# Layer 0 attention: scores of two key tiles, then the products of the last two

## Chip, cores and metric

One core of a Trainium2 chip runs the whole program. The metric is device time in microseconds (us) of one execution. Before the change it is 3277.91 us, the median of 3 runs (3275.79 to 3279.31).

## What is computed

The program is two layers: a convolution-and-attention block (layer 0) on 8 images of 256 channels and 32x32 pixels, then an attention and expert layer on the same data (layer 1). The change is in the softmax attention of layer 0, which for each image has 4 heads of 32 query and key channels and 64 value channels over 1024 pixels:

```python
qkv = _bn(_conv1x1(x, qkv_w), qkv_g, qkv_b, qkv_m, qkv_v)
qkv = qkv.reshape(B, NH, 2 * KD + HD, N)
q, k, v = (qkv[:, :, :KD], qkv[:, :, KD:2 * KD], qkv[:, :, 2 * KD:])
attn = jnp.einsum('bhkn,bhkm->bhnm', q, k) * SCALE
attn = jax.nn.softmax(attn, axis=-1)
out = jnp.einsum('bhdm,bhnm->bhdn', v, attn).reshape(B, Cc, H, W)
pe = _bn(_dwconv3(v_img, pe_w), pe_g, pe_b, pe_m, pe_v)
out = out + pe
```

The rest of layer 0 is a norm, a 1x1 convolution to 1024 channels, a 3x3 depthwise convolution, a gated product, a 1x1 convolution back and a filter on 8x8 blocks in the frequency domain.

## The kernel before

**Attention of one image** (`attend(b)`, from L725). The 1024 queries go in 4 chunks of QC = 256, the keys in NT = 8 tiles of 128, so an image has 32 steps (chunk, key tile). A step writes the scores of all 4 heads into one PSUM tile `s` (4 matmuls of 128x256, one for each head), ScalarE takes the exponential into `pT` in SBUF, and `product` multiplies the `pT` of the step before with v (8 matmuls into `po`, 32 columns each, so four can stand side by side in the array) and with ones (4 such matmuls into `sm`, for the sums of the softmax). The products are thus one step late. In the profile these are `s<-qst,kst`, `pT<-s`, `po<-pT,vT` and `sums<-pT,ones`.

**Close of a chunk** (`close`): ScalarE copies `po` to `pu` and `sm` to `ss`, then, as small steps in the list `todo` of which each step of the loop takes one (`later()`): `invert` (reciprocal `sr` on VectorE), `split` (`rh` on ScalarE, `rl` on GpSimd) and `spread` (4 matmuls `rb` on TensorE, then two VectorE operations, `pu<-pu,rb` and `o<-o,pu`).

**Other work beside it.** `main_of(i)` weaves into the steps of `attend(i)` the second norm of image i-1 (`norm2`), the frequency filter of image i-2 (`spectrum`: `pz`, `zf`, `pf`, `gf`, `py`) and the first norm and q, k of image i+1 (`queries_keys`: `nsum`, `ms`, `tr`, `rbn`, `pq`). `together` adds the depthwise convolutions as a side stream: for every microsecond that the main stream names in its `yield`, side steps worth 1.0 us (0.5 in image 0) are issued. A side step is one tap of the convolution on VectorE (`conv<-hpad`, `x<-hpad`, `o<-vpad`, 1.3 us each in its `yield`); after the third and fifth tap of a group the next group is opened: two matmuls `ph` into one PSUM bank, and two ScalarE evictions (into `hpad` and into the group's start).

**Order.** All engines here are called through `InOrder`, which keeps each engine's instructions in the order in which the Python program issues them. So the yields decide who stands behind whom in each engine's queue.

**Buffers.** PSUM has `ps_s` with 2 tiles of 2 banks (`s`, but also `pz` and others), `ps_o` with one `po` and one `sm`, and `ps_m` with 2 single banks (`ph`, `pq`, `pf`, `py`, `rb`, `rbn`, `ms`, `nsum`, `tr` and others). `pT` has 2 buffers. A tile that takes a buffer waits until the last reader of the tile that had it is done.

**End of an image** (`ending`): value products and transposes, projection, rest of the last close. After the last image comes a tail of layer 0 (to about 1400 us), then layer 1, which the change doesn't touch.

Of the kernel before, what the change touches and what calls it, by code (L numbers as in the profile page):

```python
# [9 lines left out]
F32 = mybir.dt.float32  # L10
F32R = mybir.dt.float32r
BF16 = mybir.dt.bfloat16
AF = mybir.ActivationFunctionType
# [5 lines left out]
P = 128  # L19
# [4 lines left out]
NH, KD, HD = 4, 32, 64  # L24
# [4 lines left out]
QC = 256  # L29
# [44 lines left out]
def conv_attn_hybrid_kernel(  # L74
# [351 lines left out]
    pe, act, dve, pool = (InOrder(tc, e) for e in (nc.tensor, nc.scalar, nc.vector, nc.gpsimd))  # L426
    t = [None] * B
    with ExitStack() as l0:
        wpool = l0.enter_context(tc.tile_pool(name="w0", bufs=1))
        one = l0.enter_context(tc.tile_pool(name="one0", bufs=1))  # L430
        two = l0.enter_context(tc.tile_pool(name="two0", bufs=2))
        ps_s = l0.enter_context(tc.tile_pool(name="ps_s0", bufs=2, space=PSUM))
# [289 lines left out]
        def attend(b):  # L722

            qst, kst, vT = (att[b][n] for n in ("qst", "kst", "vT"))
            nj = NT
            todo = []

            def product(po, sm, j, pT):  # L730


                for pair in range(NH // 2):
                    for i in range(4):
                        ch = pair * P + i * KD
                        pe.matmul(
                            po[i * KD : (i + 1) * KD, pair, :],
                            vT[:, j, ch : ch + KD],
                            pT[:, ch // HD, :],
                            start=(j == 0 and pair == 0),  # L740
                            stop=(j == nj - 1 and pair == 1),
                        )
                for hd in range(NH):
                    pe.matmul(
                        sm[hd * KD : (hd + 1) * KD, :], ones[:, :KD], pT[:, hd, :], start=(j == 0), stop=(j == nj - 1)
                    )

            def close(c, po, sm):
                pu = two.tile([P, NH // 2, QC], F32, tag="pu", name="pu", bufs=1)
                act.copy(pu, po)  # L750
                ss = two.tile([P, QC], F32, tag="ss", name="ss", bufs=1)
                act.activation(ss, sm, AF.Copy, accum_out=accs[:, 0, b, c : c + 1])
                r = two.tile([P, QC], F32, tag="sr", name="sr", bufs=1)
                rh = two.tile([P, QC], F32R, tag="rh", name="rh", bufs=1)
                rl = two.tile([P, QC], F32R, tag="rl", name="rl", bufs=1)
                qs = slice(c * QC, (c + 1) * QC)

                def invert():
                    dve.reciprocal(r, ss)

                def split():
                    act.activation(rh, r, AF.Copy, accum_out=accs[:, 1, b, c : c + 1])
                    pool.tensor_sub(rl, r, rh.bitcast(F32))

                def spread():
                    rb = ps_m.tile([P, NH // 2, QC], F32, tag="mm", name="rb")
                    for pair in range(NH // 2):
                        pe.matmul(rb[:, pair, :], pick_r[:, pair, :], rh, start=True, stop=False)
                        pe.matmul(rb[:, pair, :], pick_r[:, pair, :], rl, start=False, stop=True)
                    o = att[b]["o"][:, :, qs]  # L770
                    dve.tensor_mul(pu, pu, rb)
                    dve.tensor_add(o, o, pu)

                return [None, invert, None, split, None, None, spread]

            def later():
                if todo:
                    step = todo.pop(0)
                    if step:
                        step()  # L780

            late = None
            for c in range(N // QC):
                qs = slice(c * QC, (c + 1) * QC)
                po = ps_o.tile([P, NH // 2, QC], F32, tag="po", name="po")
                sm = ps_o.tile([P, QC], F32, tag="sm", name="sums")
                for j in range(nj):
                    ks = slice(j * P, (j + 1) * P)
                    s = ps_s.tile([P, NH, QC], F32, tag="s", name="s")
                    for hd in range(NH):  # L790
                        pe.matmul(s[:, hd, :], kst[:, hd, ks], qst[:, hd, qs], start=True, stop=True)
                    pT = two.tile([P, NH, QC], F32, tag="pT", name="pT")
                    act.activation(pT, s, AF.Exp)
                    if late:
                        product(*late[:4])
                        if late[2] == nj - 1:
                            todo = close(c - 1, *late[:2])
                    late = (po, sm, j, pT)
                    later()
                    yield 2.4  # L800
            product(*late)
            todo = close(c, po, sm)
            att[b]["rest"] = todo
            yield 1.3

# [224 lines left out]
        def weave(main, side, every, rest=True):  # L1030

            for n, us in enumerate(main):
                yield us
                if n % every == every - 1:
                    step = next(side, None)
                    if step is not None:
                        yield step
            if rest:
                yield from side

        def none():
            yield from ()

        def later_on(n, steps):
            for _ in range(n):
                yield 0.0
            yield from steps
# [35 lines left out]
        def main_of(i):  # L1083

            steps = attend(i)
            if i >= 1:
                head = weave(norm2(i - 1), spectrum(i - 2) if i >= 2 else none(), 1)  # L1090
                yield from weave(head, steps, 3, rest=False)
            later = queries_keys(i + 1) if i + 1 < B else none()
            yield from weave(steps, later_on(2, weave(set_up(), later, 1) if i == 0 else later), 2)
            if i + 1 < B:
                stack(i + 1)
                yield from ending(i)
            else:
                yield from weave(project(i, (0,)), weave(finish(i), gelu_steps(i - 1), 1), 1)
                yield from project(i, (1,))
# [4 lines left out]
        steps = queries_keys(0)  # L1104
# [22 lines left out]
        product, take, turn = values(0)  # L1127
# [10 lines left out]
        def set_up():  # L1138

            fold(projw, proj_s, KC, "diag_p")  # L1140
            yield 1.0
            through(piw, "n2b", 2 * ng, pi_o)
            dve.tensor_mul(dw_o, pi_o, dw_w[:, :, 4])
            yield 3.5
            fps = ps_m.tile([P, HALF], F32, tag="mm", name="fps")
            pe.matmul(fps[:, :C], sel, fp, start=True, stop=True)
            dve.tensor_copy(filt, fps[:, :C])
            yield 0.5
# [32 lines left out]
        head = weave(norm2(B - 1), spectrum(B - 2), 1)  # L1181
# [131 lines left out]
    with ExitStack() as l1:  # L1313
        wpool = l1.enter_context(tc.tile_pool(name="w1", bufs=1))
        one = l1.enter_context(tc.tile_pool(name="one1", bufs=1))
        two = l1.enter_context(tc.tile_pool(name="two1", bufs=2))
        tiny = l1.enter_context(tc.tile_pool(name="tiny1", bufs=4))
        ps_s = l1.enter_context(tc.tile_pool(name="ps_s1", bufs=2, space=PSUM))
# [136 lines left out]
        done, late, ready, turns, pr_of, pT = set(), [], [], [], {}, {}  # L1455
# [61 lines left out]
        def product(b, qc):  # L1517
            po = ps_m.tile([P, KC, QC], F32, tag="mm", name="po1")
            nj = (qc + 1) * nq
            w = pT.pop((b, qc))  # L1520
            for g in range(KC):
                for j in range(nj):
                    c0 = max(0, j * P - qc * QC)
                    pe.matmul(
                        po[:, g, c0:], v_of[b][:, j, g * P : (g + 1) * P], w[:, j, c0:], start=(j == 0), stop=(j == nj - 1)
                    )
                yield 0.43 * nj
            tb = t[b][:, :, qc * QC : (qc + 1) * QC]
            dve.tensor_add(tb, tb, po)
            done.add((b, qc))  # L1530
# [50 lines left out]
    with ExitStack() as l2:  # L1581
# [162 lines left out]
        def close(h, b, c):  # L1744

            t = ts.pop((h, b))
            dve.tensor_add(c[:, 0:2, :], c[:, 0:2, :], c[:, 7:8, :].to_broadcast([P, 2, QC]))
            dve.tensor_add(c[:, 2:4, :], c[:, 2:4, :], c[:, 1:2, :].to_broadcast([P, 2, QC]))
            dve.tensor_add(c[:, 2, :], c[:, 2, :], c[:, 6, :])
            dve.tensor_add(c[:, 4, :], c[:, 4, :], c[:, 3, :])  # L1750
            dve.tensor_add(c[:, 6, :], c[:, 6, :], c[:, 3, :])
            t4 = t.rearrange("p k (c n) -> p (k c) n", n=QC)
            dve.tensor_add(t4, t4, c[:, 0::2, :])
            nc.sync.dma_start(ov[b][:, :, cut(h)], t)
# [62 lines left out]
        for n in range(len(pieces) + LAG3):  # L1817
            one_ = two_ = three = iter(())
            if n < len(pieces):
                h, b, e = pieces[n]  # L1820
                i = n // NE
# [141 lines left out]
```

## Time and profile before

| | us |
|---|---|
| median of 3 runs | 3277.91 |
| the profiled execution | 3277.43 |
| its span, first to last instruction | 3275.3 |
| layer 0 with its tail | about 1400 |
| one image in the middle (key loads of two images 160.5 apart) | 160.5 |
| in one such image: TensorE busy | 150.95 |
| VectorE busy | 135.41 |
| ScalarE busy | 88.75 |

A window of the trace gives the busy time of each engine in it; the timeline gives the instructions one after the other, with the idle time of the engine before each and the instruction that ended this idle time. Matmul ends in the trace are modelled and overlap the next start, so distances from start to start are what counts on TensorE.

### The profile page before, as it was taken

How to read it: one execution, taken by the hardware profiler on the slowest of the kernel's cores; microseconds unless marked ns; L12 is line 12 of the kernel's file. 1: busy time of each engine (PE TensorE's matmuls, PEld its weight loads, DVE VectorE, ACT ScalarE, POOL GpSimd, SP SyncE). 2: the span in 40 equal slices, each digit the busy share in tenths (PEclk: the TensorE clock that was granted, in tenths of full speed). 3: DMA queues.
4: the chain of work that ended last, by engine and by line, in shares of the span. 5: the costliest groups of instructions: out<-in, count | busy, mean ns of one | idle time of the engine just before them, and what ended most of it. 6: DMA issues, size and time to landing. Idle time of an engine off the chain costs nothing.

```text
span 3275.3 us, 43158 instructions
## 1 busy us (share of the span) xinstructions
PE 3047.3 (93%) x17218; PEld 2050.7 (63%) x17218; DVE 2417.4 (74%) x3796; ACT 1438.2 (44%) x2227; POOL 327.9 (10%) x472
## 2 busy tenths in 40 slices
PE   7997999999999997779999998899999999999999
PEld 4554555555555554346556665678787777787787
DVE  5388888888888886735555444688888878888887
ACT  4554555555555553223333322444444444444443
POOL 2110212111111100011222111000000000000000
PEclk9998999999999999889999999999999999999999
DMA  3202020202020200031111101200000100000000
GB/s 111 53 1 52 27 52 27 53 27 52 27 52 27 52 14 20 4 136 44 50 61 51 39 26 72 75 20 20 20 20 20 33 20 20 20 20 26 20 7 13
DMA packets 49831, 121.45 MB, mean 37 GB/s; under 512 B 7302, under 2 KB 20054, under 8 KB 45782
## 3 DMA queue, kind: packets, MB, share of 16 engines
q1 hardware_dynamic: 49622, 118.61, 11.6%
q8 instruction: 137, 2.24, 0.3%
q14 instruction: 72, 0.59, 0.1%
HBM read 48.20 MB, written 37.88 MB: 26 GB/s over the span
## 4 chain that ended last, share of the span: by engine, by line
PE 48%; DVE 6%; ACT 1%; issue 1%; POOL 1%; DMA 0%; SPq 0%; ACTq 0%; POOLq 0%; DVEq 0%
PE pm L68 13%; PE pa L68 12%; PE q L68 12%; PE s L68 4%; PE po L68 3%; PE pv L68 2%; PE pk L68 2%; DVE nm L68 1%; DVE pr L68 1%; DVE zt L68 1%; DVE st L68 1%; ACT pr L68 1%; PE tp L68 1%; PE tpz L68 1%; PE tpt L68 1%
## 5 line engine op out<-in xcount | busy, mean ns | idle before, releaser
L68 ACT ACTIVATE h<-h,bn_o,bn_s 128x512 f32<-128x512 f32 x384 | 308.7, 813 | 627.7 <-DVE h L68 627.6
L68 DVE SCALAR_TENSOR_TENSOR x<-hpad,vec,x 128x1024 f32<-128x1024 f32 x248 | 320.4, 1297 | 32.1 <-ACT x L68 25.9
L68 DVE SCALAR_TENSOR_TENSOR conv<-hpad,vec,conv 128x1024 f32<-128x1024 f32 x256 | 331.5, 1301 | 14.3 <-ACT conv L68 8.4
L68 PE MATMUL pm<-h,w 128*128 128x512 f32 (+1 forms) x768 | 321.5, 528 | 0.0
L68 ACT ACTIVATE pT<-s 128x1024 f32<-128x1024 f32 x256 | 261.5, 1024 | 128.1 <-PE s L68 127.0
L68 PE MATMUL po<-pT,vT 128*32 128x256 f32 x4096 | 276.7, 388 | 12.0 <-ACT pT L68 11.3
L68 PE MATMUL ph<-xn,piw 128*128 128x512 f32 x512 | 250.8, 615 | 22.7 <-ACT conv L68 14.2
L68 PE MATMUL s<-kk,z 128*128 128x512 f32 x512 | 242.0, 600 | 0.6 <-DVE pr L68 0.6
L68 PE MATMUL s<-qst,kst 128*128 128x256 f32 x1024 | 216.5, 334 | 0.0
L68 PEld LDWEIGHTS s<-qst,kst 128*128 128x128 f32 x1024 | 146.5, 191 | 88.5 <-issue 82.2
L68 PEld LDWEIGHTS pm<-h,w 128*128 128x128 f32 x768 | 146.9, 191 | 76.6 <-issue 62.6
L68 DVE TENSOR_TENSOR h<-pa,first 128x512 f32<-128x512 f32 x128 | 88.3, 689 | 136.0 <-PE pa L68 134.3
L68 ACT ACTIVATE hpad<-ph,pi_o 128x512 f32<-128x512 f32 x126 | 87.0, 690 | 228.5 <-PE ph L68 228.4
L68 DVE TENSOR_TENSOR h<-h,wb 128x1024 f32<-128x1024 f32 x128 | 156.2, 1221 | 41.0 <-ACT h L68 41.0
L68 DVE SCALAR_TENSOR_TENSOR o<-vpad,pe_w,o 128x1024 f32<-128x1024 f32 x128 | 163.6, 1283 | 17.4 <-ACT o L68 14.7
L68 DVE TENSOR_TENSOR h<-h,first 128x256 f32<-128x256 f32 x384 | 163.2, 425 | 13.2
L68 PEld LDWEIGHTS ph<-xn,piw 128*128 128x128 f32 x512 | 88.9, 190 | 132.1 <-issue 89.1
L68 PE MATMUL pz<-pow__117,hid 128*128 128x256 f32 x512 | 129.2, 408 | 44.4 <-DVE hid L68 44.4
L68 PEld LDWEIGHTS po<-pT,vT 128*32 128x32 f32 x4096 | 107.5, 109 | 97.1 <-ACT pT L68 15.2
L68 PE MATMUL sums<-pT,ones 128*32 128x256 f32 x2048 | 158.7, 382 | 0.0
L68 PE MATMUL pa<-tz,ws 128*128 128x256 f32 x512 | 155.0, 385 | 3.8 <-DMA ws<-sums_d 3.8
L68 PE MATMUL q<-t,ws 128*128 128x256 f32 x512 | 152.8, 380 | 0.8 <-DVE t L68 0.8
(279 smaller groups left out, 5870.6 us busy)
## 6 DMA issues: line engine op xcount, KB each, us to landing
td<-t SPq DMA_DIRECT2D x8, 1024.0 KB, 3.8
t<-td SPq DMA_DIRECT2D x8, 1024.0 KB, 4.8
te<-ud SPq DMA_DIRECT2D x16, 512.0 KB, 4.0
out_dram<-te SPq DMA_DIRECT2D x16, 512.0 KB, 2.8
ze<-zd SPq DMA_DIRECT2D x15, 512.0 KB, 3.9
t<-in_x_dram SPq DMA_DIRECT2D x7, 1024.0 KB, 6.3
qst<-hi SPq DMA_DIRECT2D x56, 128.0 KB, 2.3
qst<-lo SPq DMA_DIRECT2D x56, 128.0 KB, 2.3
```

What stands on the lines that cost most here:

```text
L68: return self._tc.keep_in_program_order(method(*args, **kwargs))
```

## The change

The loop goes over pairs of key tiles. The scores of both tiles are issued first; then come, tile by tile, the products of a tile of the last pair and the exponential of the new tile. The yield is 4.8 instead of 2.4 for each tile, so that side work comes between pairs and not between tiles. The list `todo` is shortened so that `spread` still comes at about the same tile, and the weaving counts are adapted (6 norm steps for each pair instead of 3 for each tile, and every step of the loop instead of every second).

```diff
-                return [None, invert, None, split, None, None, spread]
+                return [None, invert, split, spread]
...
-            late = None
+            late = []
...
-                for j in range(nj):
-                    ks = slice(j * P, (j + 1) * P)
-                    s = ps_s.tile([P, NH, QC], F32, tag="s", name="s")
-                    for hd in range(NH):
-                        pe.matmul(s[:, hd, :], kst[:, hd, ks], qst[:, hd, qs], start=True, stop=True)
-                    pT = two.tile([P, NH, QC], F32, tag="pT", name="pT")
-                    act.activation(pT, s, AF.Exp)
-                    if late:
-                        product(*late[:4])
-                        if late[2] == nj - 1:
-                            todo = close(c - 1, *late[:2])
-                    late = (po, sm, j, pT)
+                for j0 in range(0, nj, 2):
+                    pair = []
+                    for j in (j0, j0 + 1):
+                        ks = slice(j * P, (j + 1) * P)
+                        s = ps_s.tile([P, NH, QC], F32, tag="s", name="s")
+                        for hd in range(NH):
+                            pe.matmul(s[:, hd, :], kst[:, hd, ks], qst[:, hd, qs], start=True, stop=True)
+                        pair.append((j, s))
+                    last, late = late, []
+                    for i, (j, s) in enumerate(pair):
+                        if last:
+                            product(*last[i])
+                        pT = two.tile([P, NH, QC], F32, tag="pT", name="pT")
+                        act.activation(pT, s, AF.Exp)
+                        late.append((po, sm, j, pT))
+                    if last and j0 == 0:
+                        todo = close(c - 1, *last[1][:2])
                     later()
-                    yield 2.4
-            product(*late)
+                    yield 4.8
+            for step in late:
+                product(*step)
             todo = close(c, po, sm)
+            todo.insert(2, None)
...
-                yield from weave(head, steps, 3, rest=False)
+                yield from weave(head, steps, 6, rest=False)
...
-            yield from weave(steps, later_on(2, weave(set_up(), later, 1) if i == 0 else later), 2)
+            yield from weave(steps, later_on(1, weave(set_up(), later, 1) if i == 0 else later), 1)
```

## The prediction

> **What bounds the kernel now.** I read the page first, then a table of windows for one image in the middle of layer 0, then the timeline inside it.
>
> ```profile
> PE 3047.3 (93%) x17218; PEld 2050.7 (63%) x17218; DVE 2417.4 (74%) x3796; ACT 1438.2 (44%) x2227; POOL 327.9 (10%) x472
> ```
> ```profile
> 450.40:610.90 160.50, 150.95 (x1216) 85.71 (x1214) 135.41 (x129) 88.75 (x134) 26.51 (x32) 0.99 0.15 40
> ```
>
> The columns of the second are window, length, then busy us of PE, PEld, DVE, ACT, POOL, clock, DMA share, GB/s. PE is busy 94% of an image and DVE 84%: either can set the time, in different stretches. The next lines, the PE timeline of a stretch of image 0 without side work, price a step.
>
> ```profile
> 61.14 0.74 PE L68 MATMUL s<-qst,kst 128*128 128x256 f32 x4
> 61.81 1.07 PE L68 MATMUL po<-pT,vT 128*32 128x256 f32 x16
> 62.70 0.61 PE L68 MATMUL sums<-pT,ones 128*32 128x256 f32 x8
> 63.24 0.74 PE L68 MATMUL s<-qst,kst 128*128 128x256 f32 x4
> 63.91 1.07 PE L68 MATMUL po<-pT,vT 128*32 128x256 f32 x16
> ```
>
> Start to start: a step takes 63.24 - 61.14 = 2.10. Where scores follow scores they start 0.115 apart (eight in 44.21 to 45.13), so four stream 0.46, yet `po` starts 0.67 after them: 0.21 is lost going from 128*128 to 128*32. `po` streams 0.89. `sums` followed by `nsum`, which is 128*32 too, takes 0.43 (76.27 to 76.70), followed by scores 0.54: 0.11 lost going back. So a change of shape and back costs 0.32, and 2.10 = 0.46 + 0.21 + 0.89 + 0.43 + 0.11.
>
> The third view is the timeline of all engines in that middle image.
>
> ```profile
> 546.89 0.69 DVE L68 TENSOR_TENSOR pu<-pu,rb 128x512 f32<-128x512 f32 x1 [2.94 <-PE rb L68]
> ...
> 576.12 0.69 DVE L68 TENSOR_TENSOR pu<-pu,rb 128x512 f32<-128x512 f32 x1 [1.16 <-PE rb L68]
> ...
> 596.45 1.29 DVE L68 TENSOR_TENSOR hid<-x,conv 128x512 f32<-128x512 f32 x2
> 597.77 0.78 ACT L68 ACTIVATE conv<-ph,dw_o,vec 128x512 f32<-128x512 f32 x1 [2.60 <-DVE hid L68]
> 598.60 1.98 PE L68 MATMUL ph<-xn,piw 128*128 128x512 f32 x4 [2.84 <-ACT conv L68]
> ```
>
> Until the first `rb` PE is late and DVE waits for it (2.94); afterwards DVE is full and in the end PE waits for DVE, through ACT (2.84). So the path of a middle image is PE up to the first `rb`, DVE from there to `hid`, then both.
>
> **What the Trainium skill says.** "TensorEngine Tiling (Array Packing)", Tiling Modes: a change of tiling mode drains the array. The 0.32 above agrees. "TensorE: Matmul & The Clock Gate", Architectural detail: ScalarE and VectorE are strict FIFO; so what stands behind a waiting exponential waits too. The trace of before shows ACT evictions and exponentials in issue order only. "Perfetto Trace Analysis", Identifying the Most-Contended Engine: matmul busy time is no measure of headroom. It holds here: the 94% contain the 0.32s.
>
> **The change part by part.** No arithmetic is added or removed: 1024 `s`, 2048 `po`, 1024 `sums` matmuls and 256 exponentials stay. The order in which the two programs stand on each engine shows what moves.
>
> *Shape changes.* 32 for each image become 16: 16 x 0.32 = 5.1 for each image, 41 in all. This is a gain of PE alone.
>
> *A new wait, of the exponentials.* With two `pT` buffers the exponential of a tile takes the buffer that the product just before it reads. Before, that product had been issued a whole step earlier. Now the second exponential starts only when the second product is done. From the trace: PE to ACT takes about 0.25 after the last stream (`nsum` to `part`, 77.13 to 77.38), the exponential 1.02, ACT to PE 0.04 (50.81 to 50.85). With E the end of a pair's products, it ends at E + 1.28. The next pair's second scores overwrite the scores it reads; with no side work they would start at E + 0.11 + 0.46. They wait 0.74. Side work of X us on PE between pairs shrinks this to 0.74 - X. Behind the waiting exponential stand, on ACT, the evictions of `ph`, `pq`, `ms`, the copies of the close and so on; PE waits for these where a third `ps_m` tile is wanted.
>
> *Walk of a middle image*, t = 0 at its first `pz` (475.73 in the profile), with `ph` or `pq` 1.72, `pz` 3.45, `pf` 0.86, `py` 0.95, pair of products 2.66:
> - Head. The two score tiles now come after six norm steps. The third `pz` takes the buffer of the first scores: waits 0.6 for the exponential. Second `tr`: before, scores and products stood ahead of it; now only `pf` and `rbn`. The POOL chain for it takes 5.56 + 3.77 (484.90 to 490.46 to 494.23) from t = 8.7, so it comes at 18.1 and not 16.8: 1.3. The last `pf` waits 0.7 for an eviction. First pair of products ends 23.5, second 39.9.
> - Pair 3: one `ph`, `py`, `ph` ahead, ends 48.9. Pair 4 has nothing ahead: 0.74, ends 53.6. Before, the same eight products ended at 51.7.
> - Then `ph`; `ph nsum`; `ph ms nsum ph`. In the last, `nsum` needs the bank of `ph`, evicted behind the exponential: 1.3. First `rb` starts at 75.1. Before: 70.4. The difference: waits 4.7, one more `ph`, `nsum`, `ms` and scores ahead of it 2.9, shape changes -2.2.
> - DVE takes `pu` at 75.8 instead of 71.2 (+4.6). From there to `hid` it has 29 taps of 1.29, two `sr` of 1.75, two double `xn` of 1.40, two `lo` of 0.75, two `pu`,`o` of 1.38: 48.0. Before it took 49.55 (one tap more, one wait of 1.16). So `hid` is 3.0 late.
> - After `hid` PE has one `ph` less to do (issued earlier), fewer shape changes and not the wait for `pT` of 1.21 at 604.37; DVE has 21.1 of work to its last `sr`, where before it took 23.6 with its waits. -2.4.
> Sum: +0.6. I took every hand-over at its shortest; up to the first `rb` six new ones stand on PE's path, and at an estimated 0.1 each (PE to ACT took 0.25 above, and 0.34 from the end of the `nsum` at 550.94 to its `part` at 551.71) the image comes to +1.2. Five such images: +6.0.
>
> *Image 0.* DVE has slack, PE sets the time: 16 x -0.32 = -5.1, and the short gaps between pairs (`sps` 0.47, none, `nsum` 0.43, `fps` 0.43, `tr`, `rbn tr`, `rbn`) bring waits of 0.28, 0.74, 0.31, 0.3, 0.55, 0.3, 0.3; sum 2.8. About -2.4.
>
> *Image 1.* All its norm steps now precede the scores, and the first exponentials stand bare; three gaps are empty or one `nsum`. The first close's `sr`, on which DVE waits already (5.79 before), comes at 186.8 instead of 183.5, the first `ph` evictions later still, and DVE is full from 204 to 262. +3.2.
>
> *Image 7.* No q and k of a next image: no third `ps_m` tile. First `rb` +1.1, one tap fewer behind it -1.3, hand-overs 0.6: +0.4. Its four bare gaps lie where DVE sets the pace.
>
> *Edits at nothing.* The shorter `todo` puts `spread` at tiles 22 and 23 where it was at 22; `insert(2, None)` leaves `finish` as it was. If the cover goes (DVE waiting in front of `sr`), a pair's period, 4, is the price. SP's transfers keep their order; `qst` and `kst` loads move with the image.
>
> Sum: 6.0 - 2.4 + 3.2 + 0.4 = +7.2. On the profiled execution 3277.43 (span 3275.3 and 2.1 around it) this is 3284.6; on the median, 0.5 above it, 3285.
>
> **Unknown costs, from both sides.** Per middle image: walk without allowance +0.6; if the head's waits fall into DVE's slack (up to 2.6, `tr` and `pf` and `pz`) -2.0; if instead two more evictions hold a bank as `nsum`'s does, +3.8. I take +1.2. Image 1: +1 to +5. Image 0: -3.5 (half the gaps hidden) to -1.
>
> **Rivals.**
> - *The waits only change places* (forecast): 3277 to 3295, at 3285. Chance 0.60, of which 0.20 lies within 0.2% of the time before.
> - *The shape changes come through* (faster). PE is at 94% in the page. 41 less the gaps that are too short (3 + 2 + 5 x 0.8 + 3 = 12) is 29, and about half where DVE sets half the path: 3263. Place: PE up to the first `rb` of each image. It decides if that `rb` comes no more than 1.2 later than before, since DVE's stretch behind it is shorter by 1.5. Against it: the extra `ph` ahead of it alone costs 1.7. Chance 0.15.
> - *ACT becomes the bottleneck in order*: exponentials stand behind an eviction that waits for DVE (`hpad` for the taps of the group before), and scores behind the exponential; 4 for each of 8 images: 3310. For: such waits exist (2.60 above). Against: ACT is busy 55%. Chance 0.15.
> - *Nothing moves*: DVE's 135 of 160 hide all of it: 3278. Against: DVE waits for PE at `rb`. Chance 0.10.
>
> **How the numbers follow.** Something under 0.2% (6.6 us) can't be told from no change here. Slower: 0.40 of the forecast and 0.15 of the third, 0.55. Same: 0.20 + 0.10 = 0.30. Faster 0.15. The forecast's own range is 3277 to 3295; with half of the rivals' reach on each side 3268 to 3302 holds 8 in 10.
>
> **What would show it.** Right: `s` in runs of 8 and about 0.32 less PE for each two steps; DVE's wait at the first `pu<-rb` grows from 2.94 to about 5 in middle images; PE waits of `s` for ACT `pT` of up to 0.74; `tr` for POOL `r` 1.3; image period 161 to 163. Wrong: a period under 159, or that `pu` wait gone (second case); exponentials waiting for ACT evictions over 1 each (third). If image 0 isn't shorter, the price of a shape change is not what I took.

## The result, and where it went

The changed kernel takes 3288.15 us in the median of 12 runs (3283.96 to 3294.37), the kernel before 3278.97 beside it (12 runs, 3273.93 to 3282.12). Ratio 1.0029, 95% interval 1.0022 to 1.0037: slower by 0.3%, 9.2 us. Forecast were 3285 and 7.2 us more.

The first profile of the changed kernel fell on its slowest execution (3294.37, span 3292.6, mean clock 0.969). Its page has these rows in place of those shown of before: the engines, and the two groups that the change concerns (busy us, mean ns | idle time before them).

```profile
PE 3033.9 (92%) x17218; PEld 2076.5 (63%) x17218; DVE 2412.5 (73%) x3796; ACT 1440.9 (44%) x2225; POOL 309.3 (9%) x472
...
L68 ACT ACTIVATE pT<-s 128x1024 f32<-128x1024 f32 x256 | 260.8, 1024 | 249.9 <-PE sums L68 248.4
...
L68 PE MATMUL s<-qst,kst 128*128 128x256 f32 x1024 | 187.7, 326 | 9.6 <-ACT pT L68 9.4
```

The same two groups in the kernel before:

```profile
L68 ACT ACTIVATE pT<-s 128x1024 f32<-128x1024 f32 x256 | 261.5, 1024 | 128.1 <-PE s L68 127.0
...
L68 PE MATMUL s<-qst,kst 128*128 128x256 f32 x1024 | 216.5, 334 | 0.0
```

PE is busy 13 us less, for the same 17218 matmuls, and the time is longer. Exponentials now wait for `sums`, the last matmuls of a product, and no longer for `s`; scores wait 9.4 us for exponentials, where they waited for nothing.

A second execution (label after_again below: 3287.09, span 3285.4) lies near the median and is used for the account. The next two views are tables of windows, one window for each image, bounded by the last `t<-pp` of an image. Columns as in the prediction: window, length, busy us of PE, PEld, DVE, ACT, POOL, clock, DMA share, GB/s. First the kernel before: image 0, a middle image, image 7, and the tail of layer 0.

```profile
40.00:150.59 110.59, 104.73 (x1065) 60.19 (x1067) 42.79 (x46) 58.95 (x89) 8.11 (x18) 0.98 0.25 58
...
636.40:796.85 160.45, 150.90 (x1213) 85.71 (x1212) 135.44 (x128) 88.75 (x134) 26.51 (x32) 0.99 0.15 40
...
1117.72:1261.19 143.47, 132.16 (x1131) 76.22 (x1130) 126.63 (x118) 75.68 (x108) 12.87 (x18) 0.98 0.03 12
1261.19:1398.50 137.31, 103.84 (x359) 62.29 (x358) 94.98 (x96) 36.59 (x64) 4.32 (x14) 0.91 0.03 10
```

The same of after_again, with one middle image more:

```profile
40.00:150.41 110.41, 100.96 (x1064) 61.69 (x1066) 42.25 (x47) 58.64 (x90) 7.26 (x18) 0.98 0.25 58
...
632.16:792.43 160.27, 146.56 (x1213) 87.50 (x1212) 134.51 (x129) 89.50 (x135) 23.16 (x32) 0.99 0.15 40
952.70:1116.00 163.30, 149.56 (x1213) 88.38 (x1212) 134.51 (x129) 89.50 (x135) 23.15 (x32) 0.97 0.15 40
1116.00:1263.22 147.22, 130.75 (x1131) 78.41 (x1130) 126.05 (x117) 74.04 (x106) 12.96 (x18) 0.94 0.03 12
1263.22:1404.30 141.08, 105.36 (x359) 62.99 (x358) 96.24 (x97) 36.63 (x64) 4.33 (x14) 0.90 0.02 10
```

A middle image has 4.3 us less of PE and takes as long as before (160.27 to 160.45). Image 6 takes 3 us more than images 3 to 5 although it does the same work on every engine: its clock is 0.97 and not 0.99. Image 7, the tail and the untouched rest of the program (1876.8 before, 1881.1 now, span less the end of the tail) are 3.7, 3.8 and 4.3 longer. Of these the prediction had only +0.4 for image 7.

So the clock has to be looked at. These are windows of 3.41 us of after_again in the head of image 3:

```profile
484.73:487.29 2.56, 2.56 (x13) 2.04 (x12) 2.52 (x3) 0.26 (x1) 2.48 (x3) 1.00 0.00 0
487.29:490.70 3.41, 1.61 (x8) 0.68 (x6) 3.41 (x5) 0.73 (x3) 2.19 (x7) 1.00 0.00 0
490.70:494.11 3.41, 3.41 (x16) 3.36 (x16) 2.36 (x4) 0.00 (x0) 0.00 (x0) 0.50 0.00 0
494.11:497.53 3.42, 3.42 (x54) 1.97 (x52) 1.93 (x2) 1.39 (x2) 0.00 (x0) 1.00 0.02 5
```

and these of before in the ending of image 3:

```profile
627.45:630.87 3.42, 1.11 (x9) 0.64 (x6) 3.39 (x6) 2.25 (x5) 0.00 (x0) 1.00 0.92 209
630.87:634.28 3.41, 3.17 (x4) 1.51 (x5) 0.09 (x1) 0.04 (x1) 0.00 (x0) 0.50 0.61 137
634.28:637.69 3.41, 3.41 (x12) 2.09 (x11) 1.51 (x3) 1.29 (x2) 0.00 (x0) 1.00 0.00 0
```

The clock is full or half for a whole window. The windows lie on a fixed grid: the half-clock windows of images 3 and 6 of before start at 630.87 and 1112.15, 141 windows apart, which makes 3.4133 each. In both places the window of half clock comes after one in which PE had little to do (1.61 and 1.11 us). If PE bounds such a window, it costs half of PE's busy time in it, at most 1.7 us; so for each stretch I take half of PE's busy time in its half-clock windows as what the clock costs there, and call the remainder its length at full clock. This is an estimate, too high where PE isn't the bound.

| | before: length, clock's part, at full clock | after_again |
|---|---|---|
| image 0, from 40 | 110.6, 1.7, 108.9 | 110.4, 1.7, 108.7 |
| image 1 | 137.2, 4.6, 132.7 | 136.3, 4.1, 132.2 |
| image 2 | 188.1, 5.9, 182.2 | 185.1, 3.0, 182.1 |
| images 3 to 5, each | 160.5, 1.6, 158.9 | 160.3, 1.7, 158.6 |
| image 6 | 160.4, 1.6, 158.9 | 163.3, 4.7, 158.6 |
| image 7 | 143.5, 2.2, 141.2 | 147.2, 5.1, 142.1 |
| tail of layer 0 | 137.3, 8.2, 129.1 | 141.1, 9.7, 131.4 |
| rest of the program | 1876.8, 24.0, 1852.8 | 1881.1, 27.4, 1853.7 |

Of the 10.1 us between the two spans, the clock's part is about 8, and about 2 remain at full clock: the images up to 6 gain 2, image 7, the tail and the rest lose 4. These are two single executions. In the fourteen profiles of this case the untouched rest lasts from 1877 to 1883 us, and 1881 in a kernel with the tail and the rest of before (before_filled below); how much of its 4.3 belongs to the change is not known. That the account holds, and that the clock follows PE's idle time, was argued so far; the experiments with added matmuls tested it.

### The profile page after: what moved, and what is told of

Its sections match the earlier page's. It is cut to its first block, busy times and chain, and to the rows that moved or that the text cites. A ratio compares the mean times of both kernels' runs of the same rounds, so it can differ in the third digit from the quotient of the medians.

```text
span 3292.6 us, 43182 instructions
## 1 busy us (share of the span) xinstructions
PE 3033.9 (92%) x17218; PEld 2076.5 (63%) x17218; DVE 2412.5 (73%) x3796; ACT 1440.9 (44%) x2225; POOL 309.3 (9%) x472
## 4 chain that ended last, share of the span: by engine, by line
PE 48%; DVE 6%; ACT 1%; POOL 1%; issue 1%; DMA 1%; SPq 0%; POOLq 0%; ACTq 0%; DVEq 0%
PE pm L68 12%; PE pa L68 12%; PE q L68 11%; PE s L68 4%; PE po L68 3%; PE pv L68 2%; PE pk L68 2%; DVE nm L68 1%; DVE pr L68 1%; DVE zt L68 1%; DVE st L68 1%; ACT pr L68 1%; PE tp L68 1%; DVE h L68 1%; PE tpz L68 1%
## 5 line engine op out<-in xcount | busy, mean ns | idle before, releaser
L68 PE MATMUL s<-qst,kst 128*128 128x256 f32 x1024 | 187.7, 326 | 9.6 <-ACT pT L68 9.4
L68 PEld LDWEIGHTS s<-qst,kst 128*128 128x128 f32 x1024 | 143.5, 200 | 55.9 <-issue 31.8
L68 PEld LDWEIGHTS po<-pT,vT 128*32 128x32 f32 x4096 | 121.4, 111 | 87.5 <-issue 6.5
L68 PE MATMUL pa<-tz,ws 128*128 128x256 f32 x512 | 157.1, 389 | 3.4 <-DMA ws<-sums_d 3.4
L68 PE MATMUL pa<-tz,w 128*128 128x256 f32 x512 | 153.6, 383 | 0.0
```

Source lines behind the costliest of these rows:

```text
L68: return self._tc.keep_in_program_order(method(*args, **kwargs))
```

## The experiments

Every ratio is to the kernel before, run on the same chip beside the experiment (medians 3279.5 to 3280.0).

**Three pT buffers.**

```diff
-        pow_ = wpool.tile([P, HID // P, C], F32, name="pow_")
-        nc.sync.dma_start(pow_, po_wT.rearrange("(k p) o -> p k o", p=P))
+        pow_ = piw.rearrange("p k (g o) -> p (k g) o", o=C)
...
-                        pT = two.tile([P, NH, QC], F32, tag="pT", name="pT")
+                        pT = two.tile([P, NH, QC], F32, tag="pT", name="pT", bufs=3)
```

> The changed kernel with three pT buffers; to find the room, the weights of the 1x1 convolution back (pow_) are left out and slices of piw stand in for them. The second exponential of a pair then waits for the first product of the pair and no longer for the second. Theory of the prediction (the new wait takes the place of what the shape changes give): the waits of the scores for pT (9.4 us in all) go, evictions behind the second exponential come up to 1.3 earlier, the first rb of a middle image comes 2 or more earlier and DVE's wait at the first pu falls from 6 to under 4; 1 to 2.5 us for each image, ratio to the kernel before 0.995 to 0.999. Rival (the hold of the buffer matters little; the lost time lies in how side work is grouped and in image 0): under 4 us in all, ratio 1.001 to 1.003.

3280.86 us, ratio 1.0002 (0.9996 to 1.0009). The view is ACT's table of waits in the first 1320 us: waited for, us in total, times, longest. Three buffers:

```profile
ACT pT L68 <- PE sums L68: 73.0, 101, 2.4
ACT pT L68 <- PE s L68: 59.2, 41, 4.5
```

The changed kernel (after_again):

```profile
ACT pT L68 <- PE sums L68: 245.3, 219, 6.7
```

The wait is the buffer's, and it cost 7 us (3288.15 to 3280.86), more than the rival allowed and less than the theory asked for. The load of weights that this kernel leaves out is no part of it: the first scores come at 44.6 us, in after_again at 44.0. At full clock image 0 is 105.2 instead of 108.7, image 7 139.7 instead of 142.1, but a middle image 157.8 instead of 158.6. The first `pu` of a middle image came 0.8 earlier, not 2: that step of the theory fell. The middle images are 161.0 to 164.0 long, more than in the changed kernel, because they have 2 to 4 half-clock windows each; that took part of the gain.

**The order of before in the portions of the change.**

```diff
                 for j0 in range(0, nj, 2):
-                    pair = []
                     for j in (j0, j0 + 1):
...
-                        pair.append((j, s))
-                    last, late = late, []
-                    for i, (j, s) in enumerate(pair):
-                        if last:
-                            product(*last[i])
                         pT = two.tile([P, NH, QC], F32, tag="pT", name="pT")
                         act.activation(pT, s, AF.Exp)
-                        late.append((po, sm, j, pT))
-                    if last and j0 == 0:
-                        todo = close(c - 1, *last[1][:2])
+                        if late:
+                            product(*late[0])
+                            if late[0][2] == nj - 1:
+                                todo = close(c - 1, *late[0][:2])
+                        late = [(po, sm, j, pT)]
                     later()
                     yield 4.8
```

> The changed kernel with its yields and weaving, but the instructions of a pair in the order of before: scores, exponential, product of the tile before, for each of the two tiles in turn. So the grouping of the side work, the shorter list and the weaving counts stay, the shape changes of before come back, and the new wait is gone. Theory of the prediction (shape changes are worth 5.1 for each image on PE, and PE sets the time up to the first rb and after hid): slower than the changed kernel by 10 to 25, ratio to before 1.005 to 1.010. Rival (what the pairs save is what their wait costs, and the grouping costs the rest): the same as the changed kernel, 1.002 to 1.004. Second rival (grouping costs nothing, the loss is the wait): the same as before, 0.999 to 1.001.

3307.13 us, ratio 1.0086 (1.0073 to 1.0100): 28 us slower than before, 19 slower than the change. A middle image:

```profile
644.24:808.14 163.90, 151.85 (x1213) 86.00 (x1212) 134.65 (x128) 88.75 (x134) 23.79 (x32) 0.99 0.15 40
```

It has one half-clock window and is 162.2 at full clock. So the two halves of the change can be separated: side work in portions of 4.8 instead of 2.4, with what belongs to it (the weaving counts, and `spread` after the eighth tile of a chunk where it came after the seventh), costs 162.2 - 158.9 = 3.3 for an image; two scores and two products in a row give back 162.2 - 158.6 = 3.6. The first theory's 10 to 25 us are met, the rivals fall. How the 3.3 divides among portions, counts and `spread` was not separated.

**Set-up of image 0, and norm, q and k in every image, one pair later.**

```diff
-            yield from weave(steps, later_on(1, weave(set_up(), later, 1) if i == 0 else later), 1)
+            yield from weave(steps, later_on(2, weave(set_up(), later, 1) if i == 0 else later), 1)
```

> The changed kernel with the set-up steps in image 0 one pair later (later_on(2) in place of later_on(1)); nothing else. Before, the first set-up step came after tile 5, changed after tile 3, so this is after tile 5 again. Theory: the stall of 3.2 us where sps waits for diag_p, and the half clock that follows it, are the cause of image 0 being 1.5 longer than before: image 0 gets 4 to 6 shorter, ratio to before 1.001 to 1.002. Rival: the stall only moves, since diag_p stands behind taps on DVE whose start waits for the exponentials on ACT: within 1 us of the changed kernel, 1.002 to 1.004.

3300.17 us, ratio 1.0064 (1.0051 to 1.0078): neither. The wait of `sps` is gone. Image 0 is 108.1 at full clock, 0.6 less; counted from its first scores, which came at 45.1 us here and at 44.0 in after_again, it is 1.6 less (103.1 to 104.7). But the edit does more than its expectation says: `later_on(2, ...)` stands in every image, so the norm, q and k of each next image come a pair later too. Two middle images, and DVE's first `pu` in the second of them:

```profile
477.24:641.20 163.96, 149.27 (x1213) 88.89 (x1212) 134.91 (x128) 89.56 (x134) 22.62 (x32) 0.97 0.15 40
641.20:805.10 163.90, 149.21 (x1213) 88.91 (x1212) 134.90 (x128) 89.56 (x134) 22.60 (x32) 0.97 0.15 39
...
714.84 0.69 DVE L68 TENSOR_TENSOR pu<-pu,rb 128x512 f32<-128x512 f32 x1 [2.31 <-PE rb L68]
```

The same work, in another order on PE and DVE, takes 163.9 instead of 160.3. Of these 3.6 us, by the account, 2.9 are clock, three half-clock windows in every image instead of one, and 0.7 is the order: 159.3 at full clock instead of 158.6. The first `rb` comes 4.0 earlier than in the changed kernel, and DVE waits 2.31 for it and not 5.07 (shown further down), but the image is not shorter: an early `rb` is not enough by itself. What takes the time up again was not traced.

In windows, 163.9 is 48 x 3.4133 = 163.84, and before's 160.45 is 47 x 3.4133 = 160.43: an image that has settled on a whole number of windows meets the grid at the same places each time, and keeps its number of half-clock windows. The changed kernel's 160.27 falls short of 47 windows by 0.16, so its images creep along the grid until the window edges fall differently.

**The same kernel again.** No edit.

> The changed kernel itself, for a second profile. Theory (its middle image is a little shorter than 47 windows of the clock, so that the place of the half-clock windows in the image drifts until two or three of them fall on busy work; where that happens changes from execution to execution): images without a jump are again 160.2 to 160.3 apart, images with a jump are longer by 2 to 5, and the jumps are in other images than 5 and 6 or of another size. Rival (the jumps at images 5 and 6 belong to the program): image ends at 959.4 and 1124.3 again, within 1 us.

3287.09 us in one run. Images 3 to 5 are 160.3 long, only image 6 jumps (163.3); image 0 is 110.4 and was 113.4 in the first profile, where these two images stood out:

```profile
796.11:959.43 163.32, 149.58 (x1213) 88.56 (x1212) 134.52 (x129) 89.44 (x135) 23.15 (x32) 0.97 0.15 40
959.43:1124.26 164.83, 151.10 (x1213) 89.15 (x1212) 134.34 (x128) 89.42 (x134) 23.17 (x32) 0.96 0.15 39
```

So image 5 jumps only there, and image 6 by another amount: the jumps belong to the execution. At full clock these two come to 158.6 and 158.4, where images without a jump come to 158.6.

**`rb` one pair earlier.**

```diff
-                return [None, invert, split, spread]
+                return [None, None, invert, split, spread]
...
                 for j0 in range(0, nj, 2):
+                    later()
                     pair = []
...
-            todo.insert(2, None)
+            todo = todo[1:3] + [None] + todo[3:]
```

> The changed kernel with the close of a chunk in finer steps: one step of the list at the start of a pair and one at its end, so that split comes at the start of the third pair and spread at its end, one pair earlier than in the change; invert stays. Theory of the prediction (the late first rb makes DVE wait 5 to 6 at pu, and DVE sets the time from there to hid): that wait falls to 1 to 3, hid comes 3 earlier, 1 to 3 us for each of six images, ratio to before 0.996 to 1.000. Rival (the DVE wait is slack that the end of the image takes up again): hid earlier, but the period unchanged, 1.002 to 1.004. Second rival: rb now waits on PE for rl, and the kernel gets slower, over 1.004.

3285.20 us, ratio 1.0017 (1.0010 to 1.0023), between the theory's band and the first rival's. Two of its middle images:

```profile
637.09:794.89 157.80, 146.50 (x1213) 86.96 (x1212) 134.24 (x129) 89.44 (x135) 27.77 (x32) 0.99 0.16 41
...
955.93:1118.33 162.40, 151.08 (x1213) 89.35 (x1212) 134.45 (x128) 89.43 (x134) 27.77 (x32) 0.96 0.15 40
```

And DVE's first `pu` in the first of them:

```profile
705.30 0.69 DVE L68 TENSOR_TENSOR pu<-pu,rb 128x512 f32<-128x512 f32 x1 [1.30 <-PE rb L68]
```

The mechanism is the theory's: the wait falls to 1.30, and both are 156.1 at full clock, 2.5 less than in the change. The instructions of the two stand in the same order on PE and DVE; the first has one half-clock window, the second four, and that makes the 4.6 us between them.

**Added matmuls where PE waits**, in the kernel before, in the changed one, and in the one with the early `rb`. Their results are overwritten unread. The diff is that of the changed kernel; in the kernel before, the five stand ahead of the last `ph` of an image, and the head has none.

```diff
+        def keep_busy(ps, w, n):
+            for _ in range(n):
+                pe.matmul(ps, ident, w, start=True, stop=True)
...
+                if h == 1 and wname == "n2w":
+                    keep_busy(tr, piw[:, 0, :QC], 3)
...
+                if b >= 2 and (g, h) == (1, 0):
+                    keep_busy(ps_s.tile([P, QC], F32, tag="s", name="busy"), piw[:, 0, :QC], 5)
                 pq = ps_m.tile([P, HALF], F32, tag="mm", name="pq")
...
+                    if b + 1 < B:
+                        keep_busy(pps[0][:, :QC], piw[:, 0, :QC], 4)
```

> The kernel before with nine matmuls of 128x256 for each image whose results are overwritten unread, put where PE waits: five in front of the last ph, which waits 2.84 behind hid, four in front of the second pp, which waits 1.87 for o. Theory of the clock (each image costs its time at full clock, 158.9 in the middle, and half of PE's busy time in the windows of 3.41 us that run at half clock; such a window comes after one in which PE was busy less than about half): the one half-clock window of each middle image goes, its period falls from 160.4 to about 159, ratio to before 0.995 to 0.998. Rival (the half-clock windows do not come from PE's idle time, or the added matmuls hold up PE by what they save): 0.999 to 1.003.

> The changed kernel with such matmuls at its three idle places: three in front of the second tr of the second norm (it waits 1.46 for POOL), five in front of the third pq (2.94 behind hid), four in front of the second pp (1.88). Theory of the clock: the half-clock windows of images 2 to 6 go, every middle image is 158.5 to 159 long with no jump at images 5 and 6, ratio to before 0.994 to 0.998, and within 0.2% of before_filled. Rival (the changed kernel is slower by its waits and not by the clock): it stays slower than before_filled by 0.3% as the changed kernel is slower than before; ratio to before 1.000 to 1.004.

> rb_pair_earlier with the same twelve matmuls. At full clock its middle image was worked out at 156.1, 2.4 less than that of the change, but it paid 1.7 to 6.3 for half-clock windows in each. Theory of the clock: a middle image of 156 to 157, ratio to before 0.988 to 0.993. Rival (its images were as long as they were for another reason): the same as rb_pair_earlier, 1.000 to 1.003.

3278.41 us, 0.9997 (0.9989 to 1.0006); 3281.30 us, 1.0005 (0.9996 to 1.0014); 3270.89 us, 0.9973 (0.9966 to 0.9981). A middle image of each, in this order:

```profile
636.14:795.61 159.47, 153.26 (x1231) 88.46 (x1230) 135.46 (x129) 88.82 (x135) 26.53 (x32) 1.00 0.16 41
```

```profile
635.78:795.05 159.27, 150.06 (x1237) 90.65 (x1236) 134.52 (x128) 89.45 (x134) 23.14 (x32) 1.00 0.16 41
```

```profile
632.36:789.43 157.07, 150.01 (x1237) 90.58 (x1236) 134.25 (x128) 89.44 (x135) 27.77 (x32) 1.00 0.16 41
```

The clock is 1.00, and images 3 to 6 are equally long to 0.05 us in each kernel. This is the test of the account: the periods at full clock had been put at 158.9, 158.6 and 156.1, and come out 0.6, 0.7 and 1.0 above that. I take this as the cost of the added matmuls; it can also hold an error of the account. Before and after, 1.0005 against 0.9997, can no longer be told apart: of the 9.2 us 2.9 are left, about what the account had left at full clock. The theory of the clock holds on that point. Its ratios were too low for all three, since image 1 lost up to 2.9 us by the additions (image 1 of after_filled 139.2, of after_again 136.3), and the tail and the rest of the program kept their half-clock windows.

**Fine portions again, with pairs.**

```diff
+                    later()
+                    if fine:
+                        yield 2.4
                     last, late = late, []
...
                     later()
-                    yield 4.8
+                    yield 2.4 if fine else 4.8
```

`fine` holds outside the head of an image; the list of the close is `[None, invert, None, split, None, spread]`, later_on(2) and the count 2 are back.

> The changed kernel with a second yield in each pair, between the scores and the products, 2.4 each, the weaving counts and the list of the close as fine as before (outside the head of an image, where the spectrum needs the same PSUM tiles). PE's order becomes scores of both, side work, products of both, side work: still two shape changes for each pair, but side work in small portions as before. Theory (old_order_grouped lost 28 us by the coarse portions of side work, and the pairs got 19 of them back): the grouping's loss goes and the shapes' gain stays: 2 to 4 less for each middle image at full clock, ratio to before 0.990 to 0.997. Rival (what was lost by grouping was the late close and rb or the order in the head, which stay): as the changed kernel, 1.001 to 1.004.

3281.60 us, ratio 1.0013 (1.0006 to 1.0020): the rival's band. At full clock a middle image is 157.3, 1.3 less than in the change, where 2 to 4 were expected; most have two half-clock windows and last 160.7.

**Which gains add up.** The early `rb` in the kernel before, `[None, invert, None, split, None, spread]`, with the additions of before_filled; rb_earlier_filled with additions from image 2 on (`b >= 1`, `b >= 3` and `2 <= b < B - 1` in the three conditions); and pairs_fine with the early `rb`, `[None, invert, split, None, spread]`, and the additions.

> before_filled with spread one tile earlier (tile 13 of a chunk instead of tile 14); rb_earlier_filled did the same by a pair to the changed kernel. Theory (the early rb is worth 2 for each middle image whatever the order of scores and products, because DVE sets the time from the first rb to hid): a middle image of 157 to 158.5, 159.5 in before_filled; ratio to before 0.994 to 0.998. Rival (only the pairs leave PE the room for it): 159 to 160, ratio 0.999 to 1.001.

> rb_earlier_filled with the added matmuls only from image 2 on, since image 1 was 139.1 with them and 136.6 without. Theory: image 1 gets back 2 to 2.5, the middle images stay at 157.1; ratio to before 0.996 to 0.9975. Rival (the end of image 1 only moves): the same as rb_earlier_filled, 0.997 to 0.998.

> pairs_fine with spread a tile earlier and the added matmuls of before_filled and of the head, from image 2 on. Theory (the gains add: the small portions of side work 1.2 for each middle image, the early rb 2.4, less 0.8 for the added matmuls): a middle image of 155 to 156.5, ratio to before 0.990 to 0.995. Rival (the small portions and the early rb close the same wait of DVE at the first pu, which can be closed once): 157, ratio 0.996 to 0.998.

| | median us | ratio (95%) | middle image |
|---|---|---|---|
| before_rb_filled | 3272.88 | 0.9983 (0.9975 to 0.9991) | 158.4 |
| best_coarse | 3267.36 | 0.9967 (0.9954 to 0.9979) | 157.1 |
| best_fine | 3274.69 | 0.9988 (0.9981 to 0.9995) | 158.6 |

Of the three theories best_coarse's was met (its interval reaches into the rival's band), before_rb_filled's in the image and just not in the ratio; best_fine lies outside both bands. In the order of before the early `rb` is worth 159.47 - 158.43 = 1.0 for an image, in pairs 159.27 - 157.07 = 2.2. In both, `spread` now comes after the sixth tile of a chunk. So the pairs do pay, once `rb` comes as early as in the order of before: 1.4 for an image. In the whole program it is little, 2 us from before_rb_filled to rb_earlier_filled. best_coarse has image 1 back at 136.7 and beats both kernels. With fine portions the gains don't add; why a middle image is 1.6 longer there than in best_coarse was not found out.

## Why the prediction was right, and where it was not

*The size of the total* came out right (7.2, measured 9.2), but not by its own terms, and so by luck. At full clock the change costs 2 to 3; the clock adds the other 6 to 8, and the prediction had taken it as unchanged.

*Price of a shape change, 0.32.* The eight scores that set it have seven distances between their starts, and after the first they are 0.12 apart and not 0.115, so 0.30 is nearer. (The trace holds two records for each `po` and `sums` matmul of the program, hence the x16 and x8 in its lines.) Otherwise in line with the runs: PE's busy time falls by 4.3 for a middle image, and the pairs gain 3.6 at equal portions, where 16 of them, 4.8 to 5.1, less the cost of the new wait were to be expected. The wait alone gave back 0.8 in a middle image with three buffers, 3.5 in image 0.

*The walk of a middle image.* PE in after_again, image start 632.16:

```profile
643.59 3.72 PE L68 MATMUL pz<-pow__117,hid 128*128 128x256 f32 x16 [0.53 <-ACT pT L68]
650.32 0.27 PE L68 MATMUL tr<-ident,r 128*8 128x128 f32 x1 [1.45 <-POOL r L68]
...
684.05 0.74 PE L68 MATMUL s<-qst,kst 128*128 128x256 f32 x4 [0.54 <-ACT pT L68]
702.82 0.64 PE L68 MATMUL nsum<-sq,ones 128*32 128x256 f32 x8 [1.11 <-ACT x L68]
...
758.59 1.98 PE L68 MATMUL pq<-xn,qkvw 128*128 128x512 f32 x4 [2.94 <-ACT conv L68]
```

Forecast for the first four: 0.6, 1.3, 0.74, 1.3. Each wait is in its place. Then DVE:

```profile
709.75 0.69 DVE L68 TENSOR_TENSOR pu<-pu,rb 128x512 f32<-128x512 f32 x1 [5.07 <-PE rb L68]
756.43 1.29 DVE L68 TENSOR_TENSOR hid<-x,conv 128x512 f32<-128x512 f32 x2
```

The wait at the first `pu` was to grow to about 5 and is 5.07. That `pu` comes 77.6 after the image's start; it was 71.0 in the same image of before. That is +6.6 where +4.6 was forecast, and 1.7 of it is a half-clock window: the new waits in the head leave PE 1.61 us of work in one window, and the next one, on `py` and scores, runs at half clock. `hid` is late by 3.8 (forecast 3.0), or 2.1 without that window. The rest is shorter by 4.0 (forecast 2.4), of which 1.6 is the half-clock window that before has in its ending. The window moved from the ending to the head.

*The sum for a middle image*, +1.2, was mis-sized: -0.2 measured, -0.3 at full clock. The filled kernels, whose middle images run at full clock throughout, show where. Up to the first `pu` the change costs 5.05 (76.03 and 70.98 after the image's start), so part of the allowance of 0.6 was needed; the three terms given for the first `rb`, 4.7, 2.9 and -2.2, add up to 5.4 and not to the 4.7 that the sum used. The mis-sized term is DVE's stretch from that `pu` to `hid`: 46.7 us, where 48.0 was worked out for the same 29 taps. The durations of its instructions add up to 47.7, so about 1 of the difference is that each starts a little before the last one ends. So `hid` is 2.2 late and not 3.0. The rest is shorter by 2.4, as forecast.

*Image 0*, -2.4: -0.2, and 0.0 counted from its first scores. The failed step is the list of waits. It took the gap with `sps` as a wait of scores of 0.28, and what came was this:

```profile
55.08 0.71 PE L68 MATMUL sps<-diag_p,ones 128*128 128x128 f32 x4 [3.22 <-DVE diag_p L68]
```

Two exponentials now stand ahead of the start of the taps on ACT, DVE begins its taps later, the set-up's first step comes after tile 3 instead of 5, and so its `diag_p` stands behind taps on DVE. The prediction said that an image 0 that isn't shorter would refute the price of a shape change. It did not: the gain went into this wait. The later set-up took the wait away, and image 0, from its first scores and at full clock, was 1.6 shorter than in both kernels.

*Image 1*, +3.2: -0.9, at full clock -0.5. The first `pu` comes 55.3 after the image's start instead of 54.1, 1.2 later, where the first close was to be 3.3 late, and the last one 131.1 instead of 132.0: DVE had more room than assumed.

*Image 7*, +0.4: +3.7, of which 2.9 is clock. The first `rb` term was right: its `pu` comes 2.8 later, 1.7 of it a half-clock window at its head, so 1.1, as forecast. Wrong was the term of -1.3 for one tap less behind it: between the first `pu` and the first `hid` DVE has 31 taps in both kernels, and `hid` comes 2.6 later too. The tail's +3.8 wasn't in the sum; 1.5 of it is clock by the account. The other 2.3 can't be laid to the change: at full clock the tail is 129.8 in the first profile of the same kernel and 131.4 in after_again, and it is 130.2 in before_filled, whose tail is that of before, and 129.1 in before.

*The rivals.* "The shape changes come through" was to decide at an `rb` no more than 1.2 late; it was 4.9 late at full clock. "ACT becomes the bottleneck" was to show exponentials waiting for evictions; they wait for products. "Nothing moves" is nearest in the time at full clock, with another cause: losses and gains of 3.3 and 3.6 for an image cancel. "The waits change places" is what a middle image shows.

## What to carry to other kernels

Saving work on an engine that is busy 94% brought nothing here, since the coarser order delayed what the next engine starts from. With that hand-over moved (`rb`), the saving paid, 1.4 us for an image; in setup_later, where the order behind it changed as well, it did not. Short waits on TensorE have a second price, since a few of them together can put the following window at half clock; look at the granted clock of equal stretches before explaining why they differ. And when a kernel repeats a stage, compare its stages among themselves: where one with the same instructions in the same order takes more time, look at the clock first. An edit in a loop acts in every pass of it: compare the order of the instructions before calling two stages equal.

## What was not expected of the hardware

The Trainium skill, "TensorE: Matmul & The Clock Gate", Part 1: The HAM clock gate, describes a free-running window of 3413 ns and a clock that is full or half; the 3.4133 and the 1.00 and 0.50 here agree. It gives half clock as the state after an idle window. Here PE need not be idle: in the fourteen profiles, from 320 us to the end of layer 0, every full-clock window with PE busy less than 1.39 us was followed by one at half clock, with one exception none with more than 2.0 was (the exception had 2.71), and between these both occur. PE's ends are modelled, so the limit is not known more closely. Two waits, 1.46 and 0.34 us, made the window at 487.29.

Outside this stretch busy time alone does not decide. In image 0, in twelve of the fourteen profiles, a window filled by `thr` matmuls counts as wholly busy, and half clock follows; after_again:

```profile
64.07 3.93 PE L68 MATMUL thr<-vec,piw 128*128 128x1 f32 x32
```

```profile
64.03:67.45 3.42, 3.42 (x35) 3.38 (x31) 0.00 (x0) 1.02 (x1) 0.00 (x0) 1.00 0.00 0
67.45:70.86 3.41, 3.41 (x24) 2.73 (x27) 2.75 (x4) 0.00 (x0) 0.00 (x0) 0.50 0.02 5
```

Each of these 32 matmuls has a single column (128x1). In layer 1 windows with `lg` matmuls, which have eight, are followed by half clock in the same way. So what the clock follows may be nearer to the columns that pass than to the time that the trace calls busy. No run tested that.

The second surprise is the grid's hold on a loop: equal images settled at 160.45 us in the kernel before, and at 163.9 in old_order_grouped and in setup_later, 47 and 48 windows; and in rb_pair_earlier images with the same instructions in the same order lasted 157.8 to 162.4. That the grid causes the settling was worked out from these periods and not tested by itself; that the half-clock windows go when PE's waits are filled, and the differences between images with them, was shown.
